# First output product behind the projections in pairs with 64-row products, edges kept in their tile, and another order in the first pairs

## The chip, the core and the metric

The kernel runs on one core of one Trainium2 chip. The time is that of the device, in microseconds, for one launch; runs are repeated and their median is given. The engines are TensorE (PE in the profile, its weight loads PEld), VectorE (DVE), ScalarE (ACT), GpSimd (POOL) and SyncE (SP), which here issues nearly all transfers, one after the other.

## The reference

`x` has 4 images of 128 channels and 96 x 96 pixels. One layer is computed: a group norm, then one recurrent block over four scan orders of every image (rows, rows backwards, columns, columns backwards), a product that fuses the four, and the sum with `x`. Cut to what matters:

```python
t = grouped1x1(x, in_proj_w, in_proj_b, 4)           # 128 -> 2 x 256 channels, 4 groups
u, gate = t[:, :256], t[:, 256:]
u = depthwise_conv5(silu(u), dw_w)
s = conv1x1(u, ssm_in_w)                             # 256 -> 32
a = 0.999 + 0.0009 * sigmoid(conv1x1(u, ssm_delta_w, ssm_delta_b))
bb, cc = tanh(conv1x1(u, ssm_b_w, ssm_b_b)), tanh(conv1x1(u, ssm_c_w, ssm_c_b))
hst = scan(h -> a * h + bb * s)                      # along the sequence of 9216
u = u + conv1x1(cc * hst + ssm_d * s, ssm_out_w)     # 32 -> 256
u = grouped1x1(u * sigmoid(gate), mix_w, mix_b, 4)
y = conv1x1(u, out_proj_w, out_proj_b)               # 256 -> 128
out = x + fuse_w @ concat(y of the four orders) + fuse_b
```

All numbers are 32-bit floats.

## The kernel before

**Tiling.** There are 8 phases: for each of the 4 images first the order V, then H, and in every phase the two directions side by side (`s` = 0, 1). A phase has 6 *steps* (`NS`) of 16 lines; a sequence is cut into 4 planes (`R`, every fourth element), so that a step has 4 *pairs* of 384 elements each, a pair being the same plane of both directions. So there are 192 pairs, `t` = 0 to 191, 24 in a phase (`NP`); `t % 24` says where in its phase a pair stands, `k = t % 4` where in its step. The planes are taken in the order 1, 2, 3, 0 (`TURN`). The second three steps of a phase need values of mirrored places that the first three have already computed, so these are not computed anew (`fresh(step)` is false there): the silus (`sil`) are still in their tile or are loaded back, and gate values are loaded from `kept` in DRAM.

**Stages of a pair.** The *front* (`new_front`, L482, L492) is four products of 32 x 128 weights that give the input projection of one plane; ScalarE's silu brings it into the tile `sil` (`new_silu`, L505: the upper half of the channels; `new_stage`, L516: the lower half, into a stage tile, from which four transfers, L523, bring it into `sil`). The *taps* (`taps`, L826 and L828) are the five-tap convolution of the upper half: the first tap on ScalarE into PSUM banks 0 and 1, the other four on VectorE. The *convolution* of the lower half runs on TensorE (`conv`, weights `band`, into banks 6 and 7). For planes 0 and 3 one more tap is added by VectorE from the *lone* tile (`add_lone`, L775); for planes 1 and 2 (`single` is false: `k` = 0 and 1) there is a second group of products with only 64 rows (`conv_less`, weights `less`), and ScalarE copies the result out (`copy_u`, L801). The *projections* (`proj`, weights `main`) go into banks 4 and 5 (`PROJ`); ScalarE and POOL finish them, VectorE scans once in a step half (`scan`, L903), POOL makes the outputs of the scan (`outputs`). Six pairs later (`LAG`) the state's part comes back to 256 channels (`out_of`, L650, into banks 0 to 3, `ssm(bi, s)`), on top of `u`, which ScalarE copied there before (`under`, L662). VectorE multiplies it with the gate (`gating`, L711: a pair of them, `s` = 0, then 1). The *output product* of one direction (`accumulate`, weights `w_fin`) is eight products into one bank, a copy by ScalarE (`ys`, L944 or L946) and an addition to `acc` by POOL (L963).

**Order.** The order of every engine is written out by hand, in program order (`manual_schedule`). `start` and `pair(t)` do `t` = 0 to 5, `pair_on(t)` the rest, `tail` the end. In `pair_on`: `under(bi, 1)`, taps, `conv`, `add_lone` where single, the recurrence, the first output product (bank 4), `conv_less`, `under(bi, 0)`, `copy_u`, the second output product (bank 5), then four products of a gate or of a front in turn with the four of `out_of`, gating, the first tap of the next pair, the tanh or stage silu of banks 6 and 7, and the projections. The two output products are those of the pair that was gated just before (`waiting`). In `pair(t)` with `t` = 4 the whole front 8 is made, with `t` = 5 the fronts 9 and 10 (`whole_front`; front `i` is plane `i % 4` of step `i // 4`); from `t` = 6 on, front `t + 5`.

**The edges.** The lone tile of a step holds planes 0 and 3 of its stage. It lies in one of two places (`lone_tile`): `shared` for the steps 0 and 2 of a phase, `lone` for the others. For the mirrored half the planes come back: step 3 takes the tile of step 2 as it is, steps 4 and 5 load it (`load_lone`, L764) from `edge_sil` in DRAM, where steps 1 (`new_rest`, L537) and 0 put it. `shared` also holds early gates of the next phase: in the pairs with `t % 24` = 17 and 18 the gates of `t + 7` are made there in five parts and stored (L1125 and L1149).

**Gate inputs.** `load_gate` (L316) loads what a gate's products read, eight units ahead; in the pairs with `t % 24` = 14 to 17 it loads those of the next phase's first four pairs.

## Time and profile before

| | |
|---|---|
| runs | 1734.45, 1734.15, 1734.46 us; median 1734.45 |
| profiled execution, its own time | 1736.02 us |
| its span, first to last instruction | 1734.3 us |
| mean granted TensorE clock | 0.998 |
| DMA | 362.63 MB, mean 209 GB/s |
| projections of pair 6 start at | 80.88 us |

A row of the timeline has the start in us from the beginning of the span, the busy time of a run of like instructions in us, the engine, the line of the kernel, the operation, what it writes and reads, the number of instructions, and in brackets how long the engine was idle before and who ended that. A matmul of 32-bit floats makes two instructions in the trace. A row of the windows view has the stretch, its length, the busy time of TensorE, its weight loads, VectorE, ScalarE and POOL with their instructions, the granted clock, the DMA share and GB/s. A row of the waits view has who waited for whom, for how long in total, how often, and the longest. A row of DMA issues has the transfer, the queue, how many, the KB of one and the median us to its landing.

### The profile page before, as it was taken

To read this page: it belongs to the slowest core of one execution; us is meant where nothing else is said; L and a number is where in the kernel's file an instruction comes from. 1 tells how busy PE (TensorE), PEld (TensorE's weight loads), DVE (VectorE), ACT (ScalarE), POOL (GpSimd) and SP (SyncE) were. 2 spreads that over 40 slices of the span, in tenths; PEclk is the share of its full clock that TensorE was granted. 3 is DMA by queue.
4 is the path that set the end of the run, shared out by engine and by line. 5 is a ranking of instruction groups with operands and counts; after the bars stand their busy time and mean duration, and the time that the engine had idled before them with its cause. 6 is when DMAs were issued, how large, how long until landed. Compare 5 with 4: busy or idle time off the path is not lost.

```text
span 1734.3 us, 50199 instructions
## 1 busy us (share of the span) xinstructions
PE 1706.6 (98%) x20410; PEld 703.5 (41%) x20410; DVE 1506.4 (87%) x1508; ACT 1479.8 (85%) x2435; POOL 1478.3 (85%) x1455
## 2 busy tenths in 40 slices
PE   7999999999999999999999999999999999999998
PEld 3343344434443434444444434444344433444333
DVE  6799998888889999888888989988888888888897
ACT  4788888888888888888888888888888888888875
POOL 3589898888889988988888988989888889998887
PEclk9999999999999999999999999999999999999999
DMA  7755885358994788337797488733899538753474
GB/s 241 208 169 163 281 242 146 131 197 261 287 289 152 232 245 246 124 132 251 238 306 232 154 275 239 216 117 126 253 287 288 192 119 275 227 167 116 132 239 169
DMA packets 143140, 362.63 MB, mean 209 GB/s; under 512 B 19264, under 2 KB 85696, under 8 KB 142912
## 3 DMA queue, kind: packets, MB, share of 16 engines
q1 hardware_dynamic: 142768, 359.39, 66.7%
q8 instruction: 162, 2.65, 0.7%
q14 instruction: 66, 0.54, 0.1%
q10 hardware_dynamic: 144, 0.04, 0.0%
HBM read 197.77 MB, written 126.70 MB: 187 GB/s over the span
## 4 chain that ended last, share of the span: by engine, by line
PE 89%; DMA 4%; DVE 3%; ACT 2%; issue 1%; POOL 0%; SPq 0%; ACTq 0%; DVEq 0%; POOLq 0%
PE psum L131 72%; PE psum L650 6%; PE psum L630 5%; PE psum L492 5%; DMA kept<-shared 2%; DVE psum L828 1%; DMA sil<-shared 1%; DMA sil<-sil 1%; DVE t L903 1%; DVE u L711 1%; ACT psum L826 1%; DMA acc<-in_xr 0%; PE psum L1274 0%; ACT psum L662 0%; ACT shared L516 0%
## 5 line engine op out<-in xcount | busy, mean ns | idle before, releaser
L828 DVE SCALAR_TENSOR_TENSOR psum<-sil,small,psum 128x768 f32<-128x768 f32 x576 | 589.2, 1023 | 51.6 <-ACT psum L826 34.0
L131 PE MATMUL psum<-u,w_fin 128*32 128x384 f32 (+1 forms) x6192 | 554.6, 485 | 1.1 <-ACT ys L944 0.5
L131 PE MATMUL psum<-u,main 128*32 128x384 f32 x6144 | 537.1, 490 | 1.2 <-ACT shared L672 0.6
L711 DVE SCALAR_TENSOR_TENSOR u<-gate,psum 128x768 f32<-128x768 f32 x376 | 341.9, 951 | 137.9 <-PE psum L650 65.0
L963 POOL TENSOR_TENSOR acc<-ys,acc 128x384 f32<-128x384 f32 x375 | 441.5, 1199 | 12.5 <-ACT ys L944 1.9
L131 PEld LDWEIGHTS psum<-u,w_fin 128*32 128x32 f32 x6192 | 203.1, 109 | 307.9 <-issue 209.3
L131 PEld LDWEIGHTS psum<-u,main 128*32 128x32 f32 x6144 | 180.2, 110 | 328.7 <-issue 207.3
L662 ACT COPY psum<-u 128x768 f32<-128x768 f32 x384 | 306.2, 798 | 7.1 <-DVE u L711 4.3
L909 POOL TENSOR_TENSOR t<-t,t 64x384 f32<-64x384 f32 (+1 forms) x192 | 261.8, 1364 | 45.6 <-DVE t L903 30.8
L131 PE MATMUL psum<-sil,band 128*32 128x384 f32 x3072 | 288.3, 486 | 4.4 <-ACT shared L516 2.2
L876 POOL TENSOR_SCALAR t<-tm 64x384 f32<-64x384 f32 x191 | 180.8, 947 | 125.3 <-ACT tm L865 113.4
L650 PE MATMUL psum<-t,main 32*128 32x384 f32 x1536 | 272.1, 519 | 3.7 <-ACT psum L662 3.0
L910 POOL TENSOR_TENSOR t<-t,t 64x384 f32<-64x384 f32 (+1 forms) x192 | 237.5, 1237 | 15.1
L877 POOL TENSOR_TENSOR t<-t,tm 64x384 f32<-64x384 f32 x192 | 235.6, 1227 | 15.3
L828 DVE SCALAR_TENSOR_TENSOR u<-sil,small,psum 128x768 f32<-128x768 f32 x192 | 194.9, 1015 | 6.8
L946 ACT COPY ys<-psum 128x384 f32<-128x384 f32 x288 | 138.3, 480 | 56.9 <-PE psum L131 46.9
L826 ACT ACTIVATE psum<-sil,small 128x768 f32<-128x768 f32 x191 | 171.7, 899 | 17.5 <-DVE u L711 13.4
L131 PEld LDWEIGHTS psum<-sil,band 128*32 128x32 f32 x3072 | 106.7, 109 | 153.2 <-issue 71.1
L630 PE MATMUL psum<-x_in,wn 32*128 32x384 f32 x768 | 161.0, 497 | 0.0
L492 PE MATMUL psum<-x_in,wn 32*128 32x385 f32 x704 | 149.4, 504 | 2.2 <-ACT sil L505 2.2
L505 ACT ACTIVATE sil<-psum,bnorm 128x385 f32<-128x385 f32 x176 | 102.4, 583 | 48.7 <-PE psum L492 35.5
L666 ACT ACTIVATE gate<-psum,bnorm 128x384 f32<-128x384 f32 x168 | 97.3, 581 | 43.5 <-PE psum L630 25.3
(112 smaller groups left out, 1692.6 us busy)
## 6 DMA issues: line engine op xcount, KB each, us to landing
gate<-kept SPq DMA_DIRECT2D x106, 768.0 KB, 5.6
kept<-gate SPq DMA_DIRECT2D x82, 768.0 KB, 3.7
sil<-sil SPq DMA_DIRECT2D x32, 770.0 KB, 7.9
sil<-shared SPq DMA_DIRECT2D x240, 96.2 KB, 2.8
x_in<-in_xs SPq DMA_DIRECT2D x194, 96.2 KB, 3.2
out<-acc SPq DMA_DIRECT2D x46, 384.0 KB, 7.7
x_in<-in_xs SPq DMA_DIRECT2D x88, 192.5 KB, 5.4
acc<-in_xr SPq DMA_DIRECT2D x39, 384.0 KB, 6.9
```

Of the source, the lines that this page charges most:

```text
L131: nc.tensor.matmul(o[r, : rhs.shape[-1]], lhsT, rhs, start=start, stop=stop, skip_group_check=True)
L492: nc.tensor.matmul(bank(banks[2 * j + s])[:, : N + 1], stats[units[step * UB]["b"]][0][a, s, :], x_in[s][a, q, :], start=True, stop=True,)
L630: nc.tensor.matmul(bank(to)[:, :N], stats[un["b"]][0][r, s, :], x_in[s][r, q, off : off + N], start=True, stop=True)
L650: nc.tensor.matmul(bank(ssm(bi, s) + j)[:, :N], w_so[r, bass.ts(j, P)], z[r, :], start=(bi, s) not in seeded, stop=True, skip_group_check= ...
L662: nc.scalar.copy(psum[:, ssm(bi, s) : ssm(bi, s) + 2, :N], us[bi][:, s])
L711: nc.vector.scalar_tensor_tensor(v, g, 1.0, pz, ALU.add, ALU.mult)
L826: nc.scalar.activation(part, src, AF.Copy, scale=w_tap[:, 0:1])
L828: nc.vector.scalar_tensor_tensor(us[i][:, :, 1, :] if k == K - 1 else part, src, w_tap[:, k : k + 1], part, ALU.mult, ALU.add,)
L877: nc.gpsimd.tensor_mul(ta[0:64, p, :], tb[0:64, :], tm[0:64, :])
L909: engine.tensor_mul(ta[0:64, p, r], tb[64:P, r], ta[64:P, p, r])
L910: engine.tensor_add(tb[0:64, r], ta[0:64, p, r], tb[0:64, r])
L963: adder.tensor_add(part, y, part)
```

## The change

1. In pairs with 64-row products (`not single`; not the last) the first output product is issued at the very beginning of `pair_on`, ahead of `under(bi, 1)`: on TensorE right behind the projections of the pair before, and into bank 2 in place of bank 4. Its copy to `ys` stands on ScalarE ahead of `under(bi, 1)`, its addition on POOL where it was.
2. Edges: the lone tile of a phase's step 1 stays where it is until step 4 uses it. Step 1's two stores and step 4's load go. Step 5 still loads.
3. First pairs: in pairs 4 and 5 ScalarE copies `u` in one instruction in place of VectorE in two. Front 10 goes from pair 5 to pair 6, behind its convolution, with the stage silu ahead of the two others; pair 6 has no `under`, so its gating adds `u` on VectorE (`gating`, L710). The four products of a whole front have another order.
4. The gate inputs that were loaded at `t % 24` = 16 and 17 are loaded at 21 and 22.

```diff
@@ -496,11 +496,11 @@
 
         return one
 
-    def new_silu(i, banks):
+    def new_silu(i, banks, streams=(0, 1)):
 
         step, f = divmod(i, R)
         bn = stats[units[step * UB]["b"]][1]
-        for s in range(2):
+        for s in streams:
             q = R - 1 - PLANES[f] if s else PLANES[f]
             nc.scalar.activation(
                 sils[step][:, s, 1, q, :], bank(banks[2 + s])[:, : N + 1], AF.Silu, bias=bn[:, 1:2]
@@ -532,18 +532,18 @@
             nc.sync.dma_start(kept_front[e][PLANES[f]], stage)
             if f == R - 1:
                 keep_silu(step, 0)
-        elif st == 1:
-            if f > 1:
-                nc.sync.dma_start(edge_of(step)[f - 2], stage)
-            if f == 0 and step > 1:
-                keep_silu(step - 1, 1)
-
-    def whole_front(i, banks):
+        elif st == 1 and f == 0:
+            keep_silu(step - 1, 1)
+
+    def whole_front(i, banks, stage_first=False):
         one = new_front(i, banks)
-        for s, j in ((0, 1), (0, 0), (1, 0), (1, 1)):
+        for s, j in ((0, 1), (1, 1), (0, 0), (1, 0)):
             one(s, j)
-        new_silu(i, banks)
-        new_stage(i, banks)
+        if stage_first:
+            new_stage(i, banks)
+        new_silu(i, banks, (1, 0) if stage_first else (0, 1))
+        if not stage_first:
+            new_stage(i, banks)
         new_rest(i)
 
     def edges(step, g, j, engine):
@@ -1008,14 +1008,17 @@
                 add_lone(i, banks)
             else:
                 conv_less(i, banks, False)
-                for s in range(2):
-                    nc.vector.tensor_copy(us[i][:, s, 0, :], bank(min(banks) + s)[:, :N])
+                if t < R:
+                    for s in range(2):
+                        nc.vector.tensor_copy(us[i][:, s, 0, :], bank(min(banks) + s)[:, :N])
+                else:
+                    nc.scalar.copy(us[i][:, :, 0, :], psum[:, min(banks) : min(banks) + 2, :N])
             first_tap(i + 2)
             spots = FRONT if banks == PROJ else (5, 4, 2, 3)
             if t < R:
                 front(t + R, spots)
-            for f in {4: (8,), 5: (9, 10)}.get(t, ()):
-                whole_front(f, (4, 5, 2, 3) if banks != PROJ else (6, 7, 2, 3))
+            if t >= R:
+                whole_front(t + R, (4, 5, 2, 3) if banks != PROJ else (6, 7, 2, 3))
         recurrence(t)
         stats_chunks(t)
         load_chunks(t + 2)
@@ -1058,11 +1061,21 @@
         adder = (nc.vector, True) if last else ()
 
         mirrored(t + R)
-        if k == 0 and un["st"] == NS // 2:
-            lone[un["step"]] = lone[un["step"] - 1]
-        elif k == 0 and un["st"] > NS // 2:
+        if k == 0 and un["st"] in (NS // 2, NS // 2 + 1):
+            lone[un["step"]] = lone[un["step"] - 1 - 2 * (un["st"] - NS // 2)]
+        elif k == 0 and un["st"] == NS - 1:
             load_lone(un["step"])
-        under(bi, 1)
+        def add_next(bk):
+            return accumulate(waiting.pop(0), bk, *adder) if n else None
+
+        def settle(add):
+            if add:
+                held.append(add) if late or k == R - 1 and not last else add()
+
+        ahead_of = not single and not last
+        first = add_next(2) if ahead_of else None
+        if n:
+            under(bi, 1)
         if k in (1, 3) or late:
             for b, at in reload:
                 nc.sync.dma_start(planes(accf, at), planes(xr[b], at))
@@ -1072,6 +1085,8 @@
         new_u(i)
         taps(i, range(1, K))
         conv(i, banks, single)
+        if not n:
+            whole_front(t + R, (4, 5, 2, 3), True)
         if single:
             add_lone(i, banks)
         recurrence(t)
@@ -1082,18 +1097,14 @@
         for add in held:
             add()
         held.clear()
-        def add_next(bk):
-            if n:
-                add = accumulate(waiting.pop(0), bk, *adder)
-                held.append(add) if late or k == R - 1 and not last else add()
-
-        add_next(w[0])
+        settle(first if ahead_of else add_next(w[0]))
         if not single:
             conv_less(i, banks, False)
-        under(bi, 0)
+        if n:
+            under(bi, 0)
         if not single:
             copy_u(i, banks)
-        add_next(w[1])
+        settle(add_next(w[1]))
         spots = (6, 7, 4, 5)
         if ahead is not None:
             one = new_front(ahead, spots)
@@ -1139,9 +1150,9 @@
         if gated is not None:
             for s in range(2):
                 load_gate(2 * gated + s + UB)
-        if t % NP in (14, 15, 16, 17):
+        if t % NP in (14, 15, 21, 22):
             for s in range(2):
-                load_gate(2 * (t + 10) + s)
+                load_gate(2 * (t + (10 if t % NP < 16 else 5)) + s)
         if gated is not None:
             if gated % NP > 1:
                 nc.sync.dma_start(keep(gated), to)
```

## The prediction

> **What bounds the kernel now.** I read the page first, the chain of waits second, then single pairs in the timeline.
>
> ```profile
> span 1734.3 us, 50199 instructions
> PE 1706.6 (98%) x20410; PEld 703.5 (41%) x20410; DVE 1506.4 (87%) x1508; ACT 1479.8 (85%) x2435; POOL 1478.3 (85%) x1455
> PE 89%; DMA 4%; DVE 3%; ACT 2%; issue 1%; POOL 0%; SPq 0%; ACTq 0%; DVEq 0%; POOLq 0%
> ```
>
> TensorE is busy 98% of the span and holds 89% of the chain that ended last. No product is removed here, so a gain can only come from moments in which TensorE stands or runs badly. The busy share hides some of these, so I looked for pairs that take longer than their like. An ordinary pair of 64-row products (pair 9):
>
> ```profile
> 98.41 2.79 PE L131 MATMUL psum<-u,main 128*32 128x384 f32 x32
> 101.01 1.47 PE L131 MATMUL psum<-sil,band 128*32 128x384 f32 x16
> 102.30 1.47 PE L131 MATMUL psum<-u,w_fin 128*32 128x384 f32 x16
> 103.70 0.88 PE L131 MATMUL psum<-sil,less 64*32 64x384 f32 x16
> ```
>
> The reader is to see the order: projections of the pair before, convolution, first output product, 64-row products (the second output product follows). From `main` to `less` it is 103.70 - 98.41 = 5.29 us, without a gap: here TensorE is full and the new order can give nothing. Now three pairs that are longer (8, 28 and 21), rows of TensorE and, for 28, of its weight loads:
>
> ```profile
> 89.14 2.79 PE L131 MATMUL psum<-u,main 128*32 128x384 f32 x32
> 91.75 1.63 PE L131 MATMUL psum<-sil,band 128*32 128x384 f32 x16
> 94.59 0.88 PE L131 MATMUL psum<-sil,less 64*32 64x384 f32 x16
> ...
> 264.74 2.79 PE L131 MATMUL psum<-u,main 128*32 128x384 f32 x32
> 267.35 1.70 PE L131 MATMUL psum<-sil,band 128*32 128x384 f32 x15
> 270.50 0.88 PE L131 MATMUL psum<-sil,less 64*32 64x384 f32 x16
> ...
> 267.15 1.20 PEld L131 LDWEIGHTS psum<-sil,band 128*32 128x32 f32 x15 [0.32 <-ACT shared L516]
> ...
> 203.67 2.79 PE L131 MATMUL psum<-u,main 128*32 128x384 f32 x32
> 206.75 1.50 PE L131 MATMUL psum<-sil,band 128*32 128x384 f32 x16 [0.29 <-ACT shared L516]
> 209.47 0.88 PE L131 MATMUL psum<-sil,less 64*32 64x384 f32 x16
> ...
> 1564.57 2.79 PE L131 MATMUL psum<-u,main 128*32 128x384 f32 x32
> 1570.12 0.88 PE L131 MATMUL psum<-sil,less 64*32 64x384 f32 x16
> ```
>
> `main` to `less` is 5.45, 5.76 and 5.80 us, so 0.16, 0.47 and 0.51 too long. Two causes. In pair 21 the convolution waits for ScalarE's silu (L516), which still reads banks 6 and 7. In pairs 8 and 28, the first of a step, the convolution also waits for the transfers that filled the new `sil` tile; these waits are worked off one by one behind the silu, the column groups start staggered (15 loads and one straggler in place of blocks of four), and stay so until the next change of tile size. Of the 92 pairs of this kind, 30 are over 0.05 us too long, from pair 8 to pair 176 (5.55, the last rows): 22 first ones with about 4.6 us and 8 behind a late silu with about 3.0, **7.6 us** in all.
>
> **The first pairs.**
>
> ```profile
> 63.24 3.14 DVE L828 SCALAR_TENSOR_TENSOR psum<-sil,small,psum 128x768 f32<-128x768 f32 x3
> 65.11 0.88 PE L131 MATMUL psum<-sil,less 64*32 64x384 f32 x16
> 66.41 1.01 DVE L828 SCALAR_TENSOR_TENSOR u<-sil,small,psum 128x768 f32<-128x768 f32 x1
> 67.34 1.01 DVE L1012 COPY u<-psum 128x384 f32<-128x384 f32 x2
> 67.46 0.91 ACT L826 ACTIVATE psum<-sil,small 128x768 f32<-128x768 f32 x1 [2.43 <-DVE u L828]
> 69.03 2.92 PE L492 MATMUL psum<-x_in,wn 32*128 32x385 f32 x8 [2.18 <-ACT sil L505]
> 71.88 4.65 PE L131 MATMUL psum<-u,main 128*32 128x384 f32 x32
> 80.88 2.79 PE L131 MATMUL psum<-u,main 128*32 128x384 f32 x32
> 69.00:76.00 7.00, 6.97 (x36) 2.32 (x40) 5.29 (x5) 3.20 (x5) 2.87 (x3) 0.52 0.90 254
> ```
>
> In pair 5, front 10 waits 2.18 us for bank 2, because ScalarE hung on the tap (L826) and so ran front 9's silus late. Right after, the granted clock is 0.52 for seven microseconds (window row): the projections take 4.65 where 2.79 is usual.
>
> **The change part by part.**
>
> (a) First output product behind the projections, bank 2 (92 pairs). Instructions are the same: 8 products, one ScalarE copy, one POOL add, which keeps its place. TensorE now has 16 `w_fin` matmuls between `main` and `band`, 102.30 - 101.01 = 1.29 us, and the convolution's waits can run off beneath them; the worst lateness seen is 0.51, so it is covered with 0.8 to spare. The changes of tile size stay four. New waits: bank 2 must be free and `u` gated.
>
> ```profile
> 799.32 1.82 DVE L711 SCALAR_TENSOR_TENSOR u<-gate,psum 128x768 f32<-128x768 f32 x2 [1.03 <-PE psum L650]
> 802.39 1.48 PE L131 MATMUL psum<-sil,band 128*32 128x384 f32 x16
> 803.74 0.61 ACT L886 ACTIVATE t<-t,small 64x384 f32<-64x384 f32 x1
> 806.39 0.80 ACT L801 COPY u<-psum 128x768 f32<-128x768 f32 x1
> 807.32 0.58 PE L630 MATMUL psum<-x_in,wn 32*128 32x384 f32 x1
> ...
> 203.98 1.82 DVE L711 SCALAR_TENSOR_TENSOR u<-gate,psum 128x768 f32<-128x768 f32 x2
> ```
>
> In this ordinary pair gating ends at 801.14 and the product would start at 802.39: 1.2 us to spare. The least is ahead of pair 21, where VectorE is late: gating ends at 205.80, the product would start 2.6 us after `main`, at 206.27: 0.5. On ScalarE the copy of the product now stands ahead of `under(bi, 1)` (L662), and behind it `under(bi, 0)`, `copy_u` and the gate activations. The product would end at 802.39 + 1.29 + about 0.2 = 803.9, ScalarE is done with L886 at 804.35: 0.4 us to spare, nothing waits. Behind it the same four copies follow, so `copy_u` does not get later than 807.2. If a margin were gone, each 0.1 us would cost 92 x 0.1 = 9.2 us; as 0.4 stands against that, I hold the lower end at 0 (all lateness comes back at `copy_u`) and keep the loss as a rival; the upper end is 7.6; I take **6.5**: the first-of-step part (4.6) has no engine's lateness behind it, of the other 3.0 a third will return, since VectorE is late there too.
>
> (b) First pairs. The copy of `u` in pairs 4 and 5 goes from VectorE (1.01 us) to ScalarE (0.8, as L801); front 10 goes to pair 6, behind its convolution; pair 6 skips both `under` copies and gets two VectorE adds of some 1 us in exchange (L711's size). Followed through, with the durations of the rows:
> - Pair 4: ScalarE copies `u` behind the 64-row products, 60.4 to 61.2, and only then issues the tap, to 62.1. VectorE, rid of two copies, has done its scan by then and starts the taps of pair 5 at 62.1, not 63.24; they take 3.14 + 1.01 and end at 66.2, not 67.42.
> - Pair 5: `less` ends near 66.0, a little later as front 8's stage silu is 0.9 later: 66.2. Copy on ScalarE to 67.1, tap to 68.0, front 9's silus and stage to 70.0. TensorE: front 9 at once, then projections 5 from 67.2 (`u` copied) to 70.0 at full clock, not from 71.88; convolution 6 from 70.0 (banks 6 and 7 read) to 71.4.
> - Pair 6: front 10 from 71.5, its last product when pair 5's bank 5 is read, 71.7; stage silu first, to 73.4, the two silus to 74.4. The group of front 11 and `out_of` needs bank 4 (73.4), bank 3 (73.9) and bank 2 (74.4) and ends near 75.4: projections 6 there, not at 80.88. That is 5.4 us.
> - Pair 7: the two adds make VectorE 2 us longer, where by these steps it has some 1.3 to spare; 0.7 comes back: **4.7 us** stay.
>
> Ends: 1.2 if the low clock comes again elsewhere in the head (half of seven microseconds, 3.5, is lost) to 5.4. Front 10's four stage stores and front loads are issued by SP some 3 us later than before and wanted first by pair 8's convolution at 91.75, so they keep their cover. The other order of the four products and of the silus costs nothing by itself: it only says which bank is read first.
>
> The Trainium skill, "TensorE: Matmul & The Clock Gate" (Part 1), has the clock fall after an idle window of about 3.4 us, and counts windows that run free of the program. This trace has it fall with only 2.18 us idle, so a threshold of 3.4 us of pure idleness doesn't describe it; the new gaps of about 1 us at 72 to 75 are safe by the page, and the sum below stands; if a window with the half of it idle is enough, as the trace leaves open, the sum is 3.5 us less, which is a rival below.
>
> (c) Edges kept, gate loads moved.
>
> ```profile
> 1029.86 0.58 ACT L672 ACTIVATE shared<-psum,bnorm 128x384 f32<-128x384 f32 x1 [1.62 <-DMA kept<-shared]
> 1033.26 1.50 PE L131 MATMUL psum<-sil,band 128*32 128x384 f32 x16 [1.27 <-ACT shared L672]
> 915.31 1.82 DVE L711 SCALAR_TENSOR_TENSOR u<-gate,psum 128x768 f32<-128x768 f32 x2 [2.19 <-DMA gate<-kept]
> lone<-edge SPq DMA_DIRECT2D x11, 770.0 KB, 10.0
> edge<-lone SPq DMA_DIRECT2D x14, 385.0 KB, 6.7
> SPq L1149 <- DMA sil<-sil: 16.6, 7, 3.5
> ```
>
> 14 stores and 8 of the 11 loads go, 11.5 MB, all in SP's queue. Their time lies under TensorE; what counts is who waits. In pairs 18 and 19 of a phase the early gates' tanh waits for a store (L1149) that SP issued late: each of the seven times it stood on a transfer several places ahead, after four gate loads, of which two now go to t % 24 = 21, 22. That cost about 2.3 us at pair 115 and 0.5 or so at 19 and 67; pair 102 lost 1.4 to a gate load. Of about 5 (2.3 + 0.5 + 0.5 + 1.4, and some tenths at later phases) I take half, as the phases in between lose nothing at the same place and so show that it hangs on the traffic of the moment, **2.5**; ends 5 and, if the moved loads or another order in SP's queue make a new wait like that of pair 115, -2.3. At 21, 22 they stand ahead of the stage stores and `load_kept`, which are wanted pairs later.
>
> **Sum.** 6.5 + 4.7 + 2.5 = 13.7. The profiled execution took 1736.0 us (its span and 1.7 around it), 1.6 above the median 1734.45; 13.7 less is 1722.3, and from the median 1720.8. A long stall as at pair 115 may be missing in the runs that make the median, so I stay between: **1721.5 us**.
>
> **The rivals.**
> - The head keeps its low clock and the lateness in (a) half returns: 13.7 - 3.5 - 3.0 = 7.2 off, 1728. For it: gaps of 1 us remain in the head. 17%.
> - All of it comes, (c) too: 7.6 + 5.4 + 5 = 18, 1717. 10%.
> - The change doesn't do what it says: ScalarE, 85% busy, is the real second bound; `copy_u` becomes late by what the convolution gained, and (b) is given back by VectorE before pair 12. 1733. For it: L801 ends at 807.19, close to the gates at 807.32. Against: of those gates the first needs only bank 4. 6%.
> - Slower: the product ahead of the convolution waits for gating. Decided where gating ends after `main` does, 1.2 us later than in the row above; with 0.3 us beyond that in 92 pairs, 28 us against 14 gained: 1749. The Trainium skill ("TensorE: Matmul & The Clock Gate", queue depths) calls ScalarE's queue strictly first in, first out, which would carry such a wait into all copies behind it; the rows above have ScalarE in program order throughout. Against: even the latest row above has 0.5 to spare. 5%.
>
> **Chances.** Forecast 62%, the others as given. What this kernel's measurement tells from no change is about 0.2%, 3.5 us: faster is 62 + 17 + 10 = 89%, same 6%, slower 5%. The range reaches over the forecast, the fuller gain and most of the lesser one: 1716 to 1728.5.
>
> **What would show it.** Right: `main` to `w_fin` without a wait, `band` in blocks of four in pairs 8 and 28, all 92 stretches up to `less` alike; granted clock 1.00 from 66 to 76 us, projections 6 near 75.5; no tanh wait at pair 115. Wrong: a wait `PEld psum L131 <- DVE u L711` in numbers, ScalarE waiting for `w_fin` ahead of L662, a clock of 0.5 anywhere, or new waits for transfers at t % 24 = 20 to 23.

## The result and the profile after

| | before | after |
|---|---|---|
| median of the runs, us | 1734.3 (6 runs, 1731.0 to 1736.0) | 1724.24 (6 runs, 1721.53 to 1726.26) |
| ratio, 95% interval | | 0.994, 0.9928 to 0.9953 |
| profiled execution, its own time | 1736.02 | 1726.26 |
| mean granted TensorE clock in it | 0.998 | 1.000 |
| DMA, MB | 362.63 | 350.79 |

The kernel is 0.6% faster: 10.1 us by the medians and 9.8 by the spans of the two profiles. The forecast was 1721.5. The page of the changed kernel (span, busy time, chain by engine):

```profile
span 1724.5 us, 50000 instructions
PE 1698.2 (98%) x20410; PEld 684.5 (40%) x20410; DVE 1506.1 (87%) x1506; ACT 1490.9 (86%) x2435; POOL 1485.0 (86%) x1455
PE 94%; DVE 2%; DMA 2%; ACT 1%; issue 0%; SPq 0%; DVEq 0%; ACTq 0%
```

TensorE does the same 20410 matmuls. Its share of the chain rises from 89% to 94%, that of transfers falls from 4% to 2%: the end is more nearly TensorE's own work.

**The pairs with 64-row products.** Timeline of the changed kernel, TensorE's rows of pairs 8, 21, 28 and 176, the four of the forecast, and two of the loads of the convolution of pair 28:

```profile
84.97 2.79 PE L131 MATMUL psum<-u,main 128*32 128x384 f32 x32
87.58 1.47 PE L131 MATMUL psum<-u,w_fin 128*32 128x384 f32 x16
88.87 1.48 PE L131 MATMUL psum<-sil,band 128*32 128x384 f32 x16
90.28 0.88 PE L131 MATMUL psum<-sil,less 64*32 64x384 f32 x16
...
198.34 2.79 PE L131 MATMUL psum<-u,main 128*32 128x384 f32 x32
203.64 0.88 PE L131 MATMUL psum<-sil,less 64*32 64x384 f32 x16
...
258.88 2.79 PE L131 MATMUL psum<-u,main 128*32 128x384 f32 x32
262.77 0.13 PEld L131 LDWEIGHTS psum<-sil,band 128*32 128x32 f32 x4 [0.19 <-issue]
263.10 0.13 PEld L131 LDWEIGHTS psum<-sil,band 128*32 128x32 f32 x4 [0.19 <-issue]
264.18 0.88 PE L131 MATMUL psum<-sil,less 64*32 64x384 f32 x16
...
1555.17 2.79 PE L131 MATMUL psum<-u,main 128*32 128x384 f32 x32
1560.47 0.88 PE L131 MATMUL psum<-sil,less 64*32 64x384 f32 x16
```

`w_fin` follows `main` without a wait, and the convolution, which had one straggling group in pair 28, now loads in blocks of four. From `main` to `less` it is 5.31, 5.30, 5.30 and 5.30 us, where it was 5.45, 5.80, 5.76 and 5.55. Of the 92 stretches 90 last 5.28 to 5.31; the other two, pairs 52 and 100, are new losses (below).

**The first pairs.** The window of the forecast, from the windows view:

```profile
66.00:76.00 10.00, 8.80 (x104) 3.54 (x92) 9.64 (x11) 7.72 (x13) 9.55 (x9) 1.00 1.01 309
```

The timeline: projections 5, the weight load of the first product of the group behind front 10, projections 6, and two rows of the pair after:

```profile
67.36 2.79 PE L131 MATMUL psum<-u,main 128*32 128x384 f32 x32
73.52 0.18 PEld L492 LDWEIGHTS psum<-x_in,wn 32*128 32x128 f32 x1 [1.72 <-ACT shared L516]
75.47 0.85 PE L131 MATMUL psum<-u,main 128*32 128x384 f32 x8
...
76.45 0.96 DVE L710 TENSOR_TENSOR psum<-psum,u 128x768 f32<-128x768 f32 x1
82.53 0.80 ACT L662 COPY psum<-u 128x768 f32<-128x768 f32 x1 [0.85 <-DVE u L828]
```

The granted clock is 1.00, projections 5 take 2.79 us again (they took 4.65), and projections 6 start at 75.47 instead of 80.88, 5.41 us earlier. The group waits until the stage silu has read bank 4, at 73.5, where the forecast has 73.4. Then VectorE's two new additions (L710) make the next taps late, ScalarE's `under` waits for them, and projections 7 are only 89.14 - 84.97 = 4.17 us early: 1.24 is given back.

**Transfers.** Waits and timeline of the changed kernel. First ScalarE's tanh that had waited 1.62 us at pair 115, then two gatings that wait for kept gate values, each with the issue of that load on SP ahead of it and the output product behind. The last two rows are the second load and its gating in the kernel before:

```profile
1023.58 0.58 ACT L672 ACTIVATE shared<-psum,bnorm 128x384 f32<-128x384 f32 x1 [0.33 <-PE psum L630]
...
460.44 0.34 SPq L687 DMA_DIRECT2D gate<-kept  x1
471.12 1.82 DVE L711 SCALAR_TENSOR_TENSOR u<-gate,psum 128x768 f32<-128x768 f32 x2 [4.55 <-PE psum L131]
472.99 1.50 PE L131 MATMUL psum<-u,w_fin 128*32 128x384 f32 x16 [1.97 <-DVE u L711]
...
881.86 0.35 SPq L687 DMA_DIRECT2D gate<-kept  x1
891.76 1.82 DVE L711 SCALAR_TENSOR_TENSOR u<-gate,psum 128x768 f32<-128x768 f32 x2 [3.89 <-DMA gate<-kept]
893.64 1.50 PE L131 MATMUL psum<-u,w_fin 128*32 128x384 f32 x16 [1.31 <-DVE u L711]
...
887.60 0.77 SPq L687 DMA_DIRECT2D gate<-kept  x1
895.35 1.82 DVE L711 SCALAR_TENSOR_TENSOR u<-gate,psum 128x768 f32<-128x768 f32 x2 [1.19 <-PE psum L650]
```

The view of line 687 in the changed kernel's two places, time to landing of the one load:

```profile
DMA to landing us min/median/max: 10.6/10.6/10.6
...
DMA to landing us min/median/max: 9.8/9.8/9.8
```

460.44 + 10.6 is 471.0 and 881.86 + 9.8 is 891.7: each time the gating starts when the load has landed. (The first is put down to TensorE; by the landing it is the load.) Before, the second load took 6.9 us and landed at 894.5, 0.9 us ahead of its use. In the changed kernel it is issued 5.7 us earlier and TensorE is 6.3 us ahead there, so most of the lateness is the longer landing, 9.8 in place of 6.9 us. The early product is what waits for the gating now, as the forecast's list of bad signs has it. The waits view, sum, count and longest (its two waits for kept values are those of pairs 100 and 102):

```profile
DVE u L711 <- DMA gate<-kept: 7.0, 2, 3.9
PEld psum L131 <- DVE u L711: 5.4, 6, 2.7
```

**The account.** Differences of the starts of the projections, pair by pair, between the two profiles. Both profiled executions took longer than the medians: 1736.02 us against 1734.3, and 1726.26 against 1724.24, the longest of its six.

| where | us |
|---|---|
| up to projections 7 | -4.17 |
| 24 pairs with 64-row products, 0.13 to 0.46 each | -5.56 |
| pairs 19, 67, 115, 139, 163 and the pairs 20, 68, 116 behind them (tanh and stage silus no longer behind stores), and 30 | -5.05 |
| pairs 52, 100, 102 (kept gate values late), 2.66, 2.00 and 0.44, and 93, 0.28 | +5.38 |
| all other pairs together | -0.24 |
| the last projections, 1701.15 before and 1691.51 after | -9.64 |

The forecast counted pairs 20, 68 and 116 in (a). They stand in the third row because they are as short without part 1 (in its run below, 9.11 to 9.12 us, as here).

### The profile page after: what moved, and what is told of

The parts are those of the page before. It is cut to its first block, busy times and chain, and to the rows that moved or that the text cites. A ratio compares the mean times of both kernels' runs of the same rounds, so it can differ in the third digit from the quotient of the medians.

```text
span 1724.5 us, 50000 instructions
## 1 busy us (share of the span) xinstructions
PE 1698.2 (98%) x20410; PEld 684.5 (40%) x20410; DVE 1506.1 (87%) x1506; ACT 1490.9 (86%) x2435; POOL 1485.0 (86%) x1455
## 2 busy tenths in 40 slices
DMA packets 138948, 350.79 MB, mean 203 GB/s; under 512 B 18912, under 2 KB 85344, under 8 KB 138720
## 4 chain that ended last, share of the span: by engine, by line
PE 94%; DVE 2%; DMA 2%; ACT 1%; issue 0%; SPq 0%; DVEq 0%; ACTq 0%
PE psum L131 76%; PE psum L650 7%; PE psum L630 5%; PE psum L492 5%; DVE psum L828 1%; DMA sil<-shared 1%; DVE u L711 1%; DMA x_in<-in_xs 1%; DMA acc<-in_xr 1%; PE psum L1285 0%; DVE u L828 0%; ACT psum L662 0%; ACT psum L826 0%; DVE u L775 0%; SPq L328 0%
## 5 line engine op out<-in xcount | busy, mean ns | idle before, releaser
L711 DVE SCALAR_TENSOR_TENSOR u<-gate,psum 128x768 f32<-128x768 f32 x376 | 342.1, 951 | 132.9 <-PE psum L650 61.0
L131 PEld LDWEIGHTS psum<-u,w_fin 128*32 128x32 f32 x6192 | 190.9, 109 | 323.2 <-issue 236.0
L662 ACT COPY psum<-u 128x768 f32<-128x768 f32 x382 | 300.7, 800 | 11.3 <-DVE u L711 4.3
L131 PE MATMUL psum<-sil,band 128*32 128x384 f32 x3072 | 283.4, 486 | 1.5 <-ACT shared L516 1.4
L131 PEld LDWEIGHTS psum<-sil,band 128*32 128x32 f32 x3072 | 98.8, 109 | 151.6 <-issue 95.7
```

The source lines that it names most:

```text
L131: nc.tensor.matmul(o[r, : rhs.shape[-1]], lhsT, rhs, start=start, stop=stop, skip_group_check=True)
L662: nc.scalar.copy(psum[:, ssm(bi, s) : ssm(bi, s) + 2, :N], us[bi][:, s])
L711: nc.vector.scalar_tensor_tensor(v, g, 1.0, pz, ALU.add, ALU.mult)
```

## The experiments

Each experiment computes all of the reference. The kernel before was run again beside each of three groups (medians 1733.33, 1733.49 and 1733.57 us in 29, 20 and 26 runs); ratios are to those runs.

### The parts alone

Part 1 alone, against the kernel before:

```diff
+        ahead_of = not single and not last
+        first = add_next(2) if ahead_of else None
         under(bi, 1)
...
-        add_next(w[0])
+        settle(first if ahead_of else add_next(w[0]))
```

> Part 1 of the change alone: the first output product behind the projections, in bank 2, in pairs with 64-row products. Theory (the convolution's waits run off beneath the product): 6 to 7.6 us less than before, the stretches from main to less at pairs 8, 28 and 21 equal to that of pair 9 (5.29 us), the low clock at 68 to 75 us still there. Rival (lateness only moves to ScalarE's copies, or the product waits for gating): within 2 us of before, and waits of TensorE for L711 or L801 in place of the old ones.

Part 3 alone:

```diff
-            for f in {4: (8,), 5: (9, 10)}.get(t, ()):
-                whole_front(f, (4, 5, 2, 3) if banks != PROJ else (6, 7, 2, 3))
+            if t >= R:
+                whole_front(t + R, (4, 5, 2, 3) if banks != PROJ else (6, 7, 2, 3))
...
+        if not n:
+            whole_front(t + R, (4, 5, 2, 3), True)
```

> Part 3 alone: the first pairs. Theory: projections of pair 6 start near 75.5 us (80.88 before), granted clock 1.00 throughout, 4 to 5 us less in all, of which about 1 us is given back in pair 7. Rival (the low clock is not a matter of TensorE's idle time): the clock falls to 0.5 for one window in the head again and only 1 to 1.5 us stay.

Parts 2 and 4 alone:

```diff
-        if k == 0 and un["st"] == NS // 2:
-            lone[un["step"]] = lone[un["step"] - 1]
+        if k == 0 and un["st"] in (NS // 2, NS // 2 + 1):
+            lone[un["step"]] = lone[un["step"] - 1 - 2 * (un["st"] - NS // 2)]
...
-        if t % NP in (14, 15, 16, 17):
+        if t % NP in (14, 15, 21, 22):
```

> Parts 2 and 4 alone: edges kept, gate loads at t % 24 = 21 and 22. Theory (the moved loads stand in front of the full stretch of transfers at t % 24 = 23 to 5, and that is what makes kept gate values late at pairs 51 and 99): the waits of L711 for gate<-kept appear here too, those of pairs 19, 67 and 115 are gone, the sum is within 3 us of before either way. Rival (kept values are late only because TensorE got faster): no wait at 51 and 99, 3 to 4 us less than before.

| alone | median us (range, runs) | ratio, 95% interval |
|---|---|---|
| part 1 | 1733.94 (1731.0 to 1737.23, 12) | 1.0004, 0.9995 to 1.0014 |
| part 3 | 1730.51 (1727.87 to 1735.37, 12) | 0.9984, 0.9973 to 0.9994 |
| parts 2 and 4 | 1733.78 (1731.1 to 1742.61, 12) | 1.0016, 1.0002 to 1.003 |

By the medians, against 1733.33, the three give +0.6, -2.8 and +0.5 us, 1.7 gained in all, and together they gave 10. (By its ratio, whose interval lies above 1, the last is rather a loss of 0.2%.) So the parts are not independent. Part 3 by itself does not always keep the clock up, so its rival came in part; windows of its profile:

```profile
66.00:76.00 10.00, 8.15 (x91) 3.72 (x79) 8.43 (x10) 7.01 (x12) 9.55 (x9) 0.93 0.97 292
76.00:86.00 10.00, 10.00 (x105) 3.90 (x98) 9.66 (x12) 7.59 (x13) 8.09 (x8) 0.90 0.54 155
```

The 0.07 and 0.10 that lack in ten us each are 1.7 us of clock, half of what lacks before (0.48 of 7.0, 3.4 us), and projections 6 start at 77.59, 3.3 us early instead of 5.4. With part 1 alone the steps are in the profile: 25 pairs gain 5.4 us. But the kernel also loses 0.78, 4.20, 0.29, 2.12 and 1.35 at pairs 43, 54, 68, 91 and 100, 8.7 in all. Of the 4.20 at pair 54, 1.7 is the clock, which is 0.50 from 497.55 to 500.96, right behind a wait of the gating for kept values that ended at 493.43. Its waits view:

```profile
ACT shared L675 <- DMA kept<-shared: 5.3, 5, 1.4
DVE u L714 <- DMA gate<-kept: 4.8, 2, 3.4
```

(L675 and L714 are the lines called 672 and 711 elsewhere.) Before, these were 3.0 and 2.2 us. The time is the rival's, but not by its mechanism: the gain was made and given back to transfers.

With parts 2 and 4 alone the expectation's theory came by half. The waits of the tanh are gone (pair 115 is 2.30 us shorter), and the gating waits 7.4 us for kept gate values, with pairs 52, 100 and 148 0.85, 1.50 and 1.08 longer, though part 1 is not there. But in part 3's profile, which has neither part 2 nor part 4, pair 115 is 2.30 us shorter too, and the nine pairs of the account's third row gain 4.64 of its 5.05. Over all profiles of this document pair 115 takes 8.26 to 10.91 us in the six that store and load the edges, and 8.26 or 8.27 in the eight that keep them. So part 2 does remove these stalls, and what that is worth differs from execution to execution; the 5.05 are near the upper end.

### The gate loads and the edges taken back, one at a time

Part 4 taken back, against the changed kernel:

```diff
-        if t % NP in (14, 15, 21, 22):
+        if t % NP in (14, 15, 16, 17):
             for s in range(2):
-                load_gate(2 * (t + (10 if t % NP < 16 else 5)) + s)
+                load_gate(2 * (t + 10) + s)
```

> The whole change but for part 4: gate loads again at t % 24 = 16 and 17. Theory (the moved loads are the cause of the new waits): no wait of L711 for gate<-kept at pairs 51 and 99 (2.7 and 2.0 us in the profile of the changed kernel), the waits at 19, 67 and 115 partly back; 1 to 4 us less than the changed kernel, if the edges kept are what cured 115, else the same as it. Rival (the faster TensorE is the cause, or chance): waits at 51 and 99 stay, time not below the changed kernel's.

1724.25 us (1720.81 to 1729.15, 6 runs), ratio 0.9951, 0.9933 to 0.9969: no difference from the changed kernel. Its waits view has more of the new wait, not less, and none for `kept<-shared`:

```profile
DVE u L711 <- DMA gate<-kept: 11.7, 3, 4.8
```

So the moved loads are not needed for the kept gate values to be late, and they are not what cures the tanh at pairs 19, 67 and 115.

Part 2 taken back, against the changed kernel:

```diff
+            if f > 1:
+                nc.sync.dma_start(edge_of(step)[f - 2], stage)
...
-        if k == 0 and un["st"] in (NS // 2, NS // 2 + 1):
+        if k == 0 and un["st"] == NS // 2:
```

> The whole change with the edges of step 1 stored and loaded again; parts 1, 3 and 4 as in the changed kernel. Theory (11.5 MB less in the transfer queue is what lets the gain through): waits of ScalarE for the stores out of the shared tile come back at pairs 19, 67 or 115, 3 to 8 us lost, 1727 to 1732, ratio 0.996 to 0.999. Rival (the edges are worth nothing by themselves, the gain is that of (a) and (b)): within 2 us of the changed kernel, 1722 to 1726, ratio 0.994 to 0.995.

1724.42 us (1722.1 to 1731.16, 9 runs), ratio 0.9951, 0.9934 to 0.9969. The theory's mechanism came and its price didn't:

```profile
DVE u L714 <- DMA gate<-kept: 6.6, 3, 2.5
ACT shared L675 <- DMA kept<-shared: 3.4, 4, 1.2
```

ScalarE waits for the stores again (pair 67 is 1.23 us longer than in the changed kernel, pair 115 1.40), but pairs 52, 100 and 102 are 4.6 us shorter, 54 and 101 0.7 longer. What the edges lose at the one place doesn't reach the end, because less is lost at the other. Beside parts 1 and 3, part (c) is worth nothing that these runs can measure.

### The whole change without one of its two large parts

Without part 1, and in the third group of runs without part 3 (the lines of part 3 above, the other way round):

```diff
-        ahead_of = not single and not last
+        ahead_of = False
```

> The whole change without its part 1: the first output product stays behind the convolution, in bank 4; edges, gate loads and first pairs are as in the changed kernel. Theory (the gain of (a), 7 us step by step, is real and comes through to the end once part (c) has taken traffic away): 7 us slower than the changed kernel, about 1731 us, ratio to before 0.998, the steps at the k = 0 and 1 pairs gone, pair 6 still 5 us earlier. Rival (the end is set by transfers, and (a) only moves idle time about, as the run of part 1 alone suggests): within 2 us of the changed kernel, 1722 to 1726, ratio 0.994 to 0.995.

> The whole change without its part 3: the first pairs are as before (copies of u on VectorE, front 10 in pair 5); the early product, the kept edges and the moved gate loads stay. Theory (the parts' gains are steps at their own places, 7 us for (a), 3 to 4 for (b), and what the sum lacks is waits for late transfers, which every kernel has): 3 to 4.5 us slower than the changed kernel, 1727 to 1729, ratio to before 0.996 to 0.998, pair 6's projections 5 us later and all later steps as in the changed kernel. Rival ((a) is worth nothing without (b), as the run of part 1 alone suggests): 1733 to 1735, ratio 0.999 to 1.001, with 6 us or more of waits for transfers in the profile.

| whole change without | median us (range, runs) | ratio, 95% interval |
|---|---|---|
| part 1 | 1727.22 (1726.05 to 1737.22, 12) | 0.9968, 0.9953 to 0.9984 |
| part 3 | 1727.93 (1723.8 to 1731.38, 9) | 0.9963, 0.9950 to 0.9976 |

Within the whole, part 1 is worth 1727.22 - 1724.24 = 3.0 us and part 3 3.7. The changed kernel was not run again in these groups; with each time taken against its own group's kernel before, it is 3.8 and 4.4. The first lies between theory and rival: pair by pair the profile without part 1 lacks 5.4 us of steps at 25 pairs, but its gating also waits less (3.6 us for kept gate values, against 7.0), and pairs 52, 100 and 102 are 5.4 shorter. So by the medians some 3 of 5.4 reach the end, and by these two profiles, which end within 0.3 us of each other, none; but the one is the shortest of its twelve executions and the other the longest of its six. The second is what the theory said: part 1 does not need part 3, for beside parts 2 and 4 it takes the time from 1733.78 to 1727.93. Without part 3 the low clock is back in the head, and the waits for kept gate values are there as well (behind the one in pair 52 the clock is 0.50 once more, from 477.15 to 480.57), by the windows and the waits of its profile:

```profile
66.00:76.00 10.00, 7.46 (x61) 2.46 (x60) 8.27 (x9) 5.60 (x9) 4.46 (x6) 0.83 0.95 260
```

```profile
DVE u L711 <- DMA gate<-kept: 13.2, 4, 5.0
```

**The clock over many executions.** Every execution of these kernels has a mean granted clock to three digits. Counted:

| | executions | at 1.000 | mean |
|---|---|---|---|
| kernel before | 75 | 4 | 0.9984 |
| five kernels without part 3 | 57 | 4 | 0.9984 |
| eight kernels with part 3 | 62 | 48 | 0.9997 |

A mean higher by 0.0013 is 0.0013 x 1727 = 2.2 us of full clock. So part 3 does what it says, mostly: 14 of 62 executions still had a low clock somewhere.

### The other bank

```diff
-        first = add_next(2) if ahead_of else None
+        first = add_next(4) if ahead_of else None
```

> The changed kernel with the early output product in bank 4, where it was before, and not in bank 2. Bank 4 then still holds the projections of the pair before, which ScalarE and POOL are reading when the product wants to start. Theory (the other bank is what makes the early place free of a wait): TensorE waits at w_fin in each of the 92 pairs, for 0.1 to 0.3 us, by 9.2 us for each 0.1: 1733 to 1750 us, ratio 1.000 to 1.010. Rival (the readers of bank 4 are done in time): no wait at w_fin, 1722 to 1726, ratio 0.994 to 0.995.

1747.49 us (1746.41 to 1748.82, 6 runs), ratio 1.0078, 1.0056 to 1.0099. Timeline around the projections of pair 8, and the waits view:

```profile
95.59 2.79 PE L131 MATMUL psum<-u,main 128*32 128x384 f32 x32
97.77 0.58 ACT L865 ACTIVATE tm<-psum,small 128x384 f32<-128x384 f32 x1
98.40 1.50 PE L131 MATMUL psum<-u,w_fin 128*32 128x384 f32 x16
```

```profile
PEld psum L131 <- ACT tm L865: 74.1, 93, 1.4
```

The product starts 2.81 us behind `main`, not 2.61, when ScalarE has read bank 4 (97.77 + 0.58 = 98.35). 93 such waits cost 1747.49 - 1724.24 = 23.3 us, 0.25 each. (The waits of weight loads add up to more, because a part of each lies under the matmuls before.) This is the forecast's slower rival, with its price, for another reader: the early place pays only because bank 2 is free, and 0.2 us of lateness there in every pair would have made the change a loss.

### The kept gate values ahead of the stage

One line moved in the changed kernel, and the same edit on top of part 1 alone and in the kernel before:

```diff
+        load_kept(n + 2)
         if ahead is not None:
             new_stage(ahead, spots)
-        load_kept(n + 2)
-        if ahead is not None:
             new_rest(ahead)
```

> The changed kernel, with one line moved: the load of the kept gate values of the pair after next is issued ahead of the stage's four transfers, not behind them. Theory (the gating of pairs 51, 99, 101 or 147 waits because that load is issued late on SP, behind the stage's transfers): the waits of L711 for the kept gate values fall from 7 us in all to under 2, and the kernel is 3 to 5 us faster than the changed one, 1719 to 1721, ratio to before 0.991 to 0.993. Rival (the load is late because the transfer engines are full there, wherever it is issued): the waits stay, 1723 to 1726, ratio 0.994 to 0.995. It could also only move the wait to the stage's transfers, seen as a wait of the convolution's weight loads in the same pairs, with no gain.

> Part 1 alone, with the load of the kept gate values ahead of the stage's transfers. Theory (part 1 alone gave nothing because its 6 to 7 us were eaten by waits for transfers, of which the kept gate values took the most): 3 to 6 us faster than part 1 alone, 1728 to 1731, ratio to before 0.997 to 0.999, without waits of the gating for kept gate values; the waits of ScalarE for the stores out of the shared tile stay. Rival (the loss is that of the transfer engines being full, whichever transfer is last): 1732 to 1735, with other waits in place of those.

> The kernel before, with the load of the kept gate values ahead of the stage's transfers and nothing else changed: the control to the run above. Theory (the late load costs in the kernel before too, but less, since its TensorE is later where the load lands): 1 to 2 us faster than before, ratio 0.999. Rival 1 (the load's place is worth as much here as in the changed kernel, 2.6 us or more, so it says nothing of part 1): ratio 0.998 or less. Rival 2 (nothing, since the profile of before has one such wait of 2.2 us only): ratio 1.000.

| with the load first | median us (range, runs) | ratio, 95% interval | without it |
|---|---|---|---|
| the changed kernel | 1721.65 (1720.37 to 1725.25, 6) | 0.9932, 0.9912 to 0.9952 | 0.994 |
| part 1 alone | 1730.94 (1728.01 to 1735.39, 12) | 0.9987, 0.9976 to 0.9999 | 1.0004 |
| the kernel before | 1734.36 (1730.71 to 1743.42, 12) | 1.0006, 0.9993 to 1.0020 | 1 |

In the changed kernel the waits of L711 for kept gate values are gone: the load that was issued at 881.86 is issued at 875.09 here, 6.8 us earlier while TensorE is 2.8 us earlier in that pair, and it still takes 9.3 us to land, so the earlier issue is what cures this wait. But the profiled execution, the slowest of the six, shows what the expectation named last. Issue of that load, and the loads of the convolution of pair 100:

```profile
875.09 0.67 SPq L687 DMA_DIRECT2D gate<-kept  x1
...
892.57 0.14 PEld L131 LDWEIGHTS psum<-sil,band 128*32 128x32 f32 x2 [2.45 <-ACT ys L944]
893.51 0.14 PEld L131 LDWEIGHTS psum<-sil,band 128*32 128x32 f32 x2 [0.80 <-DMA sil<-lone]
894.03 0.14 PEld L131 LDWEIGHTS psum<-sil,band 128*32 128x32 f32 x2 [0.39 <-DMA sil<-lone]
894.55 0.20 PEld L131 LDWEIGHTS psum<-sil,band 128*32 128x32 f32 x7 [0.39 <-DMA sil<-lone]
```

Here the stage's four transfers land late, 9.4 to 12.1 us after their issue. (The first row is put down to a copy that had ended at 891.91; by the landings it waits for the first of them.) The clock is 0.50 right behind, from 894.18 to 897.59, so 1.7 of the 5.2 us that the pair loses are the clock's. The other five executions took 1720.37 to 1721.85, and no profile tells what they waited for. The median gain of 2.6 us is less than the 3 to 5 expected, and its interval overlaps that of the changed kernel, so it is likely, not proven.

On part 1 alone the edit gives 3.0 us, the low end of its theory, though the two intervals just overlap; in the kernel before it gives nothing, as its second rival has it. So the late kept values are likely what takes a good part of part 1's gain when it stands alone. Why they are late there is not settled: TensorE's lead is not enough, for in part 1's profile pair 100 loses 1.35 us with TensorE 2.6 us behind the kernel before. The waits that are left there are the stores' (`kept<-shared`, 6.9 us in 5), which kept edges remove: all six profiles that store and load the edges have waits for `kept<-shared` (0.7 to 6.9 us), none of the eight that keep them has one, and part 1 with parts 2 and 4 is at 1727.93.

### A candidate

The load first, as above, and the moved gate loads put elsewhere:

```diff
-        if t % NP in (14, 15, 21, 22):
+        if t % NP in (14, 15):
...
+        if t % NP == 6 and t > NP:
+            for s in range(4):
+                load_gate(2 * (t - 4) + s)
```

> The candidate: the changed kernel with the load of the kept gate values ahead of the stage's transfers, and the gate inputs of the phase's third and fourth pairs loaded in its seventh pair in place of t % 24 = 21 and 22, that is not right ahead of the stretch in which the transfer engines are full. Theory (those loads add to that stretch): 1 to 3 us faster than the changed kernel with the first of the two edits alone, 1718.5 to 1721, ratio to before 0.990 to 0.992, no wait over 2 us for a transfer in pairs 47 to 55 and 95 to 103. Rival (the place of these loads does not matter, as taking part 4 back did not): the same as with the first edit alone, 1721 to 1723, ratio 0.9925 to 0.994.

1722.04 us (1721.03 to 1723.75, 5 runs), ratio 0.9932, 0.9918 to 0.9946. The rival holds: the time is that of the load first alone. Its profile has no wait for a transfer over 0.7 us behind the first pairs, and yet it is the slowest of the five, because the clock fell in the first 40 us: it is 0.50 from 26.80 to 33.62, and the mean clock of the other four executions is 1.000. A window and a row of TensorE ahead of the fall, of this kernel:

```profile
20.00:40.00 20.00, 19.41 (x306) 11.61 (x308) 8.97 (x28) 12.44 (x26) 3.52 (x5) 0.83 0.49 122
...
24.98 5.14 PE L131 MATMUL psum<-x_in,wn 32*32 32x385 f32 x88 [0.59 <-DMA x_in<-in_xs]
```

The same of part 1 with the load first, whose profiled execution was its slowest too:

```profile
20.00:40.00 20.00, 19.80 (x314) 11.85 (x316) 9.18 (x28) 12.83 (x27) 3.53 (x5) 0.83 0.52 127
...
24.47 1.51 PE L131 MATMUL psum<-x_in,wn 32*32 32x385 f32 x30 [0.20 <-DMA x_in<-in_xs]
```

Projections 0 start at 39.39 and 38.87 us there, against 35.04 before and 35.29 after. The changed kernel with the load first, and the candidate, beat the kernel before, and by their medians the changed one by 2 to 3 us.

## Why the prediction was right, and where its sum was off

- **Bound and direction.** TensorE's moments of standing were the place to look: no product went, and the gain is the 4.17 us up to projections 7 and the pairs named, less what the loads took back. The range, 1716 to 1728.5, holds the time, and the sign is that of the forecast. By the medians the gain is 10.1 us where the working has 13.7.
- **(a), forecast 6.5 of 7.6.** The steps measure 5.56 in 24 pairs (5.4 against the whole change without part 1; with pairs 20, 68 and 116, which the 7.6 counted and which do not need part 1, it would be 6.6). The mechanism is as told: no wait ahead of `w_fin` and 90 of 92 stretches alike, with blocks of four in the rows shown. In those 90 the margins for gating and ScalarE held; in the other two the gating waits for a load. What the forecast left out is that a step gained does not reach the end when the next transfer is late: some 3 us do within the whole, none in part 1 alone.
- **(b), forecast 4.7.** 4.17 up to projections 7. Projections 6 were put at 75.4 and came at 75.47; the additions on VectorE gave back 1.24, not 0.7, since the lateness went on into ScalarE's copy. By the medians 3.7. The profile of the kernel before is a long one here: from projections 0 to 7 it takes 54.1 us, the five other profiles without part 3 take 53.0 to 53.2, with the low clock for 3.4 us and not 6.8, and the changed kernel 49.7. So 3.4 to 3.5 is the usual gain where the clock stays up, and it fell in the head's pairs 5 and 6 in two of the eight profiles with part 3.
- **(c), forecast 2.5.** This is the term that was mis-sized. Taking part 2 or part 4 back changes the median by 0.2 us or less (1.0 against each group's own kernel before), with intervals that overlap, so (c) is worth nothing that can be measured. The working was to halve "about 5", with the low end at -2.3 for "another order in SP's queue". The account does have 5.05 at the pairs it named and a few like them, but 4.64 of that came without (c) in part 3's profile, so it is no sure gain. And the new waits, nearly all for kept gate values, cost 5.38 in this execution, where the low end had one of 2.3. They are not (c)'s alone: at pairs 52, 100 and 102 they are 5.4 us less without part 1 and 4.6 less with the edges back. The forecast read pair 102's wait for `gate<-kept` as a thing that goes; it is one of a kind that comes in many of these kernels. By the waits views it is 2.2 to 7.4 us in the four profiles without part 1 and 4.8 to 13.2 in the five with it in bank 2, all with the load in its old place.
- **Sum.** 5.56 + 4.17 - 0.33 = 9.4, near the 9.64 of the last projections, against 13.7. As the account books it, the shortfall is 2.8 in (c), 0.9 in (a) and 0.5 in (b). That one pair of executions comes so near the 10.1 of the medians is in part luck, since each took some 2 us more than its median.
- **Rivals.** Slower by a product that waits: it needed 0.3 us in 92 pairs, and with bank 4 that came true, 0.25 us and 23 us, though behind ScalarE's reading and not the gating. ScalarE as second bound: no. The low clock: gone from the head's pairs 5 and 6 in this profile and five others with part 3, but not a thing that a program holds fixed.
- **The Trainium skill**, "TensorE: Matmul & The Clock Gate" (Part 1), was weighed for the low clock: it has the clock at half after an idle window of about 3.4 us. The length comes back in these traces, where a low stretch lasts 3.4 or 6.8 us, but not the idleness: in the 3.4 us ahead of a fall TensorE stood from 0.2 us (in the last of the rows above) to 2.8 us (with bank 4, from 71.55), and some 1.9 us without a fall in part 1 with the load first, from 1029.71. So no threshold comes out. The Trainium skill's remark that the window runs free of the program, so that one kernel behaves otherwise from run to run, is made of the ramp at the start; it fits the counts here too: 48 of 62 and 8 of 132 executions at 1.000.
- **Open.** Which transfer is late differs from execution to execution of one kernel, and one profile of each can't say how often. Why pairs 52 and 100 suffer was narrowed to the place of the load in SP's queue, since moving it cures that wait; which of the transfers ahead of it makes the difference, and why the same load takes 9.8 us to land where it took 6.9, was not tried.

## What to carry to other kernels

When an engine with 98% is sped up by tenths in many places, look next at what arrives just in time for it: the load that landed 0.9 us ahead of its use became the longest new wait, 3.9 us, and part of the gain is paid to it. Measure a change's parts inside the whole as well as alone, because a part that gives nothing alone may be worth 3 us beside others. Take the size of a stall from more than one execution before counting it as a gain: the 2.3 us at pair 115 were gone in one profile of a kernel that did nothing about them. And before moving a product ahead, choose the bank by who still reads it: with one bank the change gained 10 us, with the other it lost 14 against the kernel before of its group.

## What the runs showed of the hardware that was not expected

- A load of kept gate values that was issued 6.8 us earlier on SP took nearly as long to land (9.3 against 9.8 us), in a stretch where the DMA share is over 1 (1.03 from 875.0 to 884.4 with the load first): what moved its landing was its place in the issue order. Windows of the changed kernel over it:

```profile
872.00:881.00 9.00, 9.00 (x108) 3.87 (x101) 7.13 (x8) 8.06 (x13) 8.46 (x9) 1.00 1.05 228
881.00:890.00 9.00, 9.00 (x107) 3.91 (x108) 6.53 (x7) 7.79 (x13) 8.26 (x9) 1.00 1.06 295
```

- The granted clock can fall to 0.50 for 6.8 us (26.19 to 33.01 in part 1 with the load first) when TensorE has stood for only 0.20 us in the 3.4 us before, while it ran products of 32 x 32 weights. In the candidate the like happened in one execution and not in the four others.
- A late transfer can cost twice. Right behind such waits the clock was 0.50 for 3.4 us in three profiles (pair 54 of part 1 alone, pair 52 without part 3, pair 100 with the load first), 1.7 us more each time.
